# A two-layer graph network: the attention step over three groups, exponentials kept in PSUM, a bias by matrix product

## The chip, the cores and the metric

The kernel runs on one core of a Trainium2 chip. The metric is the device time of one execution in microseconds (us); for the kernel before it is the median of three timed runs. Five engines work side by side on their own instruction streams: TensorE (PE, with its weight loads as PEld), VectorE (DVE), ScalarE (ACT), GpSimd (POOL), and SyncE (SP), which here only starts transfers. SBUF is the on-chip memory, PSUM the small one that TensorE writes its products to.

## What is computed

The input is x, 3125 nodes of 256 features, with 50000 edges sorted by target. Each layer adds to x a graph part and a mixing part, both of the normalised x, and then a feed-forward part. Only the first half of layer 1 matters here:

```python
xn = _layernorm(x)
# graph part: attention over the edges, 4 heads, 64 features
messages = (xn @ Wf.T)[src] * direction[:, 0:1] + (xn @ Wr.T)[src] * direction[:, 1:2]
scores = leaky_relu(einsum('ef,hf->eh', messages, attn), 0.2)
exp_scores = exp(scores - scores.max(axis=0, keepdims=True))
norm = exp_scores / (segment_sum(exp_scores, dst)[dst] + 1e-10)
outs = [segment_sum(messages * norm[:, h:h+1], dst) for h in range(4)]
# mixing part ("Galerkin"): 8 heads of 64, no softmax
q, k, v = split(xn @ Wqkv.T, 3);  k, v = inst_norm(k), inst_norm(v)
dots = einsum('bhnd,bhne->bhde', k, v)
out = einsum('bhnd,bhde->bhne', q, dots) / n
x = x + concat(outs) + (out @ Wout.T + bout)
```

Everything is in float32.

## The kernel before

The 3125 nodes are 25 tiles of 125 (P = 125, NT = 25), in seven chunks (`CHUNKS`) of four, four, four, four, three, three and three tiles. The edges are 391 columns of 128, and `GROUP = 8` columns make a group: 49 groups. The program runs through layer 0's mixing (a dense adjacency that is built by scattering and multiplied, L460), layer 0's feed-forward (a mixture of experts, whose two results per token are added to x at L915, chunk by chunk, two loads and two adds each), layer 1's mixing, and layer 1's feed-forward (another mixture of experts with its own graph attention). Outside of the attention loop a framework that sees what each instruction reads and writes sets the order of each engine's instructions; it does so from the program and a model of costs.

Layer 1's mixing, `layer1_mix`, begins with `layernorm` (per tile `bn_stats` L168 and `bn_aggr` L169 on VectorE; per chunk a Sqrt on ScalarE L170, a reciprocal L171, per tile the normalised row L178 on VectorE, transposes on TensorE L183 and copies on ScalarE L185). `token_matmul` (L191, two products per tile) then makes a table of 136 numbers per node: for each of the two directions 64 message features and 4 head scores. The table `tab1` is written to device memory.

The attention loop goes over the 49 groups and two more iterations. Inside it, for TensorE, VectorE and ScalarE, the order of instructions is the order in which the program issues them (`manual_schedule`); GpSimd's and SyncE's are left to the framework. Iteration i does, in this order:

- `fetch(i+3)`: eight indirect gathers (L51, GpSimd's queue) of table rows, into one of four buffers `g1`;
- `messages(i)`: VectorE makes messages and scores (L1211 to L1215) and the group's maximum per head (L1220), TensorE transposes it (L1222, PSUM tile `psm`);
- `weigh(i-1)`: VectorE multiplies the messages of the group before with the exponential of each head (L1268, 128 x 2048 elements), which ScalarE has written into the 65th column of each head's block in `v`;
- `maximum(i)`: VectorE updates the running maximum (L1229 to L1231), TensorE spreads it over the partitions (L1235);
- `products(i-1)`: TensorE multiplies one-hot matrices of the targets with `v` (L1276), for each window of 125 targets that the group may touch, one PSUM tile `pw` per window, from four buffers. A group touches one to three windows, and so has 8 to 16 columns to multiply;
- `add(i-2)`: VectorE rescales the window's accumulator by how the maximum grew (L1285) and adds `pw` (L1287); for a window met for the first time ScalarE copies it (L1290);
- `ones_of(i)`: VectorE makes the one-hot matrices (L1260); `exponents(i)`: VectorE subtracts the maximum (L1240, L1241), ScalarE makes the exponentials (L1243, and L1245 for the growth).

At the end of every iteration the generator `galerkin` is advanced once by `next(todo, None)`, and so lays the mixing part between the groups. Its steps, one per iteration: the key and value weights are loaded, transposed (L1446, copied at L1447) and centred (L1451 to L1453); then 26 kv steps. Step t normalises tile t-1 (sum of squares L1462, L1463, L1465 on VectorE, Sqrt L1466 on ScalarE, reciprocal L1467 and multiply L1468 on VectorE), adds it into `pdots` (L1470, TensorE, four products), and makes keys and values of tile t (TensorE L191, copies L1480 and squares L1482 on ScalarE). Then come one step for `dots` and the transposed `Wout`, one for `m2` (L1502, L1503), and one for the combined matrix `gm` (L1511, L1513) with the first of seven chunks; a chunk multiplies each tile of xn with `gm` (L191), adds the product to x (L1519, VectorE), and after its last tile adds the bias, spread over all partitions, to the chunk (L1520, VectorE). The remaining six chunks take one step each.

Of the kernel before, what the change touches and what calls it, by code (L numbers as in the profile page):

```python
# [18 lines left out]
D = 256  # L19
P = 125  # L20
NT = 25
# [4 lines left out]
GROUP = 8  # L26
# [62 lines left out]
class Kernel:  # L89
# [1068 lines left out]
    def layer1_mix(self):  # L1158
        nc, tc, a = self.nc, self.tc, self.a
        W, HD = 68, 64  # L1160
        with ExitStack() as m:
            big = m.enter_context(tc.tile_pool(name="l1", bufs=1))
            wk = m.enter_context(tc.tile_pool(name="l1w", bufs=2))
            gp = m.enter_context(tc.tile_pool(name="l1g", bufs=3))
            ps_a = m.enter_context(tc.tile_pool(name="l1pa", bufs=2, space=PSUM))
            ps_c = m.enter_context(tc.tile_pool(name="l1pc", bufs=1, space=PSUM))
            ps_w = m.enter_context(tc.tile_pool(name="l1pw", bufs=4, space=PSUM))
            ps_s = m.enter_context(tc.tile_pool(name="l1ps", bufs=1, space=PSUM))

            xT = big.tile([128, 2, N], F32, name="xT2")  # L1170
# [67 lines left out]
            def exponents(n, s, pb):  # L1238
                big2 = gp.tile([128, 2, 4], F32, name="top_b", bufs=4)
                nc.vector.tensor_copy(big2, pb)  # L1240
                nc.vector.tensor_sub(s[:, :n, :], s[:, :n, :], big2[:, 0:1, :].to_broadcast([128, n, 4]))  # L1241
                v = gp.tile([128, GROUP, 4, HD + 1], F32, name="v1", bufs=2)
                nc.scalar.activation(v[:, :n, :, HD], s[:, :n, :], AF.Exp)  # L1243
                grown = gp.tile([128, 4], F32, name="grown", bufs=4)
                nc.scalar.activation(grown, big2[:, 1, :], AF.Exp)  # L1245
                return big2, grown, v

            def tiles_in(j0, n):

# [14 lines left out]
                    hots.append(hot)  # L1264
                return hots

            def weigh(n, o, v):
                nc.vector.tensor_mul(v[:, :n, :, :HD], o[:, :n, None, :HD].to_broadcast([128, n, 4, HD]),  # L1268
                                     v[:, :n, :, HD:].to_broadcast([128, n, 4, HD]))

            def products(j0, n, v, hots):
                sums = []
# [23 lines left out]
            with tc.manual_schedule(engines={E_.PE, E_.DVE, E_.Activation}):  # L1296
                todo = self.galerkin(big, wk, ps_a, ps_c, xT)
                starts = [(j0, min(GROUP, NJ - j0)) for j0 in range(0, NJ, GROUP)]
                G = len(starts)
                ahead = [fetch(starts[i][0]) for i in range(3)]  # L1300
                msg, exps, summed = {}, {}, {}
                for i in range(G + 2):
                    if i + 3 < G:
                        ahead.append(fetch(starts[i + 3][0]))
                    if i < G:
                        j0, n, g = ahead[i]
                        o, s, pt = messages(j0, n, g)
# [12 lines left out]
                last = exps[G - 1][0]  # L1320
# [14 lines left out]
            for t0, n in CHUNKS:  # L1335
                s = slice(t0, t0 + n)
# [96 lines left out]
    def galerkin(self, big, wk, ps_a, ps_c, xT):  # L1433

        nc, a = self.nc, self.a
        wkv = big.tile([128, 2, 1024], F32, name="wkv")
        for c4 in range(2):
            nat = wk.tile([128, 4, D], F32, name="nat4", bufs=1)  # L1440
# [14 lines left out]

        pc = ps_c.tile([128, 4, 128], F32, name="pdots")
        kvs = {}
        for t in range(NT + 1):
            if t > 0:
                kv, sq = kvs.pop(t - 1)  # L1460
                var = wk.tile([P, 16], F32, name="kv_var")
                nc.vector.tensor_reduce(var, sq, AX.X, OP.add)  # L1462
                nc.vector.tensor_scalar(var, var, 1.0 / 64, LN_EPS, op0=OP.mult, op1=OP.add)  # L1463
                both = wk.tile([P, 8], F32, name="kv_both")
                nc.vector.tensor_mul(both, var[:, 0:8], var[:, 8:16])  # L1465
                nc.scalar.activation(both, both, AF.Sqrt)  # L1466
                nc.vector.reciprocal(both, both)  # L1467
                nc.vector.tensor_mul(kv[:, 8:, :], kv[:, 8:, :], both[:, :, None].to_broadcast([P, 8, 64]))  # L1468
                for hp in range(4):
                    nc.tensor.matmul(pc[:, hp, :],  # L1470
                                     kv[:, 8 + 2 * hp:10 + 2 * hp, :].rearrange("p a b -> p (a b)"),
                                     kv[:, 2 * hp:2 * hp + 2, :].rearrange("p a b -> p (a b)"),
                                     start=(t == 1 and hp == 0), stop=(t == NT and hp == 3),
                                     skip_group_check=True)
# [12 lines left out]
        for s in (slice(0, 64), slice(64, 128)):  # L1487
            nc.vector.tensor_copy(dots[s, :, s], pc[s, :, s])

        woT = big.tile([128, 4, D], F32, name="woT")  # L1490
        nat = wk.tile([128, 2, 512], F32, name="nat4", bufs=1)
        nc.sync.dma_start(nat, a["L1_mix_Wout"].rearrange("(c p) f -> p c f", p=128))
        for cc in range(2):
# [2 lines left out]
                nc.tensor.transpose(pt[:, i, :], nat[:, cc, i * 128:(i + 1) * 128], self.ident)  # L1496
            nc.scalar.copy(woT[:, :, cc * 128:(cc + 1) * 128], pt)
        yield
        m2 = big.tile([128, 4, D], F32, name="m2")
        for hp in range(4):  # L1500
            pm = ps_a.tile([128, D], F32, name="ln_pt")
# [2 lines left out]
        wq = wk.tile([128, 4, D], F32, name="nat4", bufs=1)  # L1504
        nc.sync.dma_start(wq, a["L1_mix_Wqkv"][0:512, :].rearrange("(c p) d -> p c d", p=128))
        yield
        g = big.tile([128, 2, D], F32, name="gm")
        for k in range(2):
            pm = ps_a.tile([128, D], F32, name="ln_pt")
# [1 line left out]
                nc.tensor.matmul(pm, wq[:, hp, k * 128:(k + 1) * 128], m2[:, hp, :],  # L1511
                                 start=(hp == 0), stop=(hp == 3))
            nc.scalar.copy(g[:, k, :], pm)  # L1513
        bout = self.bcast(big, "L1_mix_bout")
        for t0, n in CHUNKS:
            for t in range(t0, t0 + n):
                pm = ps_a.tile([P, D], F32, name="ln_pt")
                self.token_matmul(pm, xT, t, g)
                nc.vector.tensor_add(self.x[:, t, :], self.x[:, t, :], pm)  # L1519
            nc.vector.tensor_add(self.x[:, t0:t0 + n, :], self.x[:, t0:t0 + n, :],  # L1520
                                 bout[:, None, :].to_broadcast([P, n, D]))
            yield


# [386 lines left out]
```

## Time and profile before

| | us |
|---|---|
| timed runs: median (lowest, highest) | 3240.6 (3229.06, 3284.13) |
| profiled execution, its own time | 2833.29 |
| profiled execution, span | 2831.5 |
| mean granted TensorE clock | 0.874 of full speed |
| attention: first messages to last messages | 1632.7 to 2233.7 |

Busy time in some stretches of the profiled execution, with the mean granted clock:

| stretch, us | what runs | PE | DVE | ACT | POOL | clock |
|---|---|---|---|---|---|---|
| 1550 to 1633 | last adds of layer 0, layernorm, table | 27.6 | 35.1 | 17.9 | 9.2 | 0.63 |
| 1700 to 1900 | groups with kv steps | 180.9 | 181.5 | 92.5 | 158.7 | 1.00 |
| 1900 to 2000 | last kv steps, `dots`, `m2`, `gm` | 80.3 | 81.5 | 31.1 | 79.5 | 0.91 |
| 2000 to 2120 | groups with chunks | 81.3 | 67.2 | 4.7 | 70.9 | 0.82 |
| 2120 to 2250 | groups alone | 102.8 | 114.5 | 7.5 | 86.7 | 0.86 |

How to read the lines of a profile: L1268 is line 1268 of the kernel. A group of instructions names its line, engine and operation, then what it writes, an arrow and what it reads, the shape (partitions x elements) and how many there are. A line of a single instruction, or of a run of equal ones, begins with its start and its duration in us, and ends with the engine's idle time just before it and what ended it, in square brackets. A line of waits names who waits, for whom, and the total in us, the number of waits and the longest. The clock digits give the granted TensorE clock in tenths for forty equal slices of the span, 9 being 90% or more. The profiled execution is 407 us shorter than the median of the timed runs.

### The profile page before, as it was taken

To read this page: it belongs to the slowest core of one execution; us is meant where nothing else is said; L and a number is where in the kernel's file an instruction comes from. 1 tells how busy PE (TensorE), PEld (TensorE's weight loads), DVE (VectorE), ACT (ScalarE), POOL (GpSimd) and SP (SyncE) were. 2 spreads that over 40 slices of the span, in tenths; PEclk is the share of its full clock that TensorE was granted. 3 is DMA by queue.
4 is the path that set the end of the run, shared out by engine and by line. 5 is a ranking of instruction groups with operands and counts; after the bars stand their busy time and mean duration, and the time that the engine had idled before them with its cause. 6 is when DMAs were issued, how large, how long until landed. Compare 5 with 4: busy or idle time off the path is not lost. (4 is left out here: it accounts for less than half of the span.)

```text
span 2831.5 us, 26589 instructions
## 1 busy us (share of the span) xinstructions
PE 2184.2 (77%) x9023; PEld 1643.4 (58%) x9023; DVE 1529.5 (54%) x3663; ACT 523.4 (18%) x1051; POOL 1673.8 (59%) x1493
## 2 busy tenths in 40 slices
PE   1761759999976999999998369988668676999900
PEld 1450547876663677888887346665556554666600
DVE  7975598545569501222121479988558841322227
ACT  2320000000011112222221224443000021222300
POOL 4888788773003604666665077777748417777740
PEclk9855869999967999999999679999888878999955
DMA  8920533312401205555553421112111121122242
GB/s 299 382 89 14 115 89 89 87 44 71 112 31 31 74 1 202 191 191 185 183 184 113 105 62 48 48 47 54 46 32 45 27 68 16 25 52 51 58 89 68
DMA packets 179598, 263.46 MB, mean 93 GB/s; under 512 B 54398, under 2 KB 144008, under 8 KB 176193
## 3 DMA queue, kind: packets, MB, share of 16 engines
q1 hardware_dynamic: 121008, 204.78, 23.4%
q0 software_dynamic: 52544, 47.72, 7.4%
q10 hardware_dynamic: 5894, 9.09, 1.0%
q8 instruction: 75, 1.23, 0.2%
q14 instruction: 77, 0.63, 0.1%
HBM read 177.15 MB, written 84.22 MB: 92 GB/s over the span
## 5 line engine op out<-in xcount | busy, mean ns | idle before, releaser
L58 POOL DMA_INDIRECT adj<-ch_sum,ch_place x391 | 513.3, 1313 | 148.3 <-issue 111.5
L51 POOL DMA_INDIRECT g<-tab,t_src x391 | 458.6, 1173 | 222.5 <-issue 109.4
L58 POOL DMA_INDIRECT sorted<-s_rows,pos x256 | 245.9, 960 | 186.7 <-DVE s_rows L1055 118.2
L460 PE MATMUL psum<-sup,adjT 125*125 125x256 f32 x1250 | 292.8, 393 | 52.4 <-DMA adjT<-adj 41.2
L1276 PE MATMUL pw<-v,hot 128*125 128x260 f32 x1244 | 320.5, 420 | 0.0
L51 POOL DMA_INDIRECT G<-tabg,g_src x256 | 254.2, 993 | 79.9 <-issue 70.4
L460 PEld LDWEIGHTS psum<-sup,adjT 125*125 125x125 f32 x1250 | 240.8, 194 | 94.0 <-DMA adjT<-adj 43.3
L1276 PEld LDWEIGHTS pw<-v,hot 128*125 128x125 f32 x1244 | 253.7, 207 | 48.0
L864 PE MATMUL ph<-xs,w 128*128 128x256 f32 x1024 | 231.5, 384 | 8.5 <-issue 6.0
L892 PE MATMUL py<-w,h 128*128 128x256 f32 x1024 | 231.2, 379 | 0.0
L864 PEld LDWEIGHTS ph<-xs,w 128*128 128x128 f32 x1024 | 193.6, 192 | 45.7 <-issue 17.6
L1632 PE MATMUL fpy<-fw,fh 128*125 128x256 f32 x800 | 186.2, 389 | 32.2 <-DVE y L1634 27.1
L892 PEld LDWEIGHTS py<-w,h 128*128 128x128 f32 x1024 | 192.1, 190 | 24.8
L1632 PEld LDWEIGHTS fpy<-fw,fh 128*125 128x125 f32 x800 | 152.2, 192 | 70.1 <-DVE y L1634 28.4
L866 ACT ACTIVATE h<-ph,b 128x256 f32<-128x256 f32 x256 | 121.3, 475 | 366.2 <-PE ph L864 335.8
L1624 PE MATMUL fph<-xT,fw 128*128 128x500 f32 (+1 forms) x448 | 176.4, 543 | 0.3 <-DMA fw<-in_L_ffn_W_dram 0.3
L1030 PE MATMUL pctx<-s_mv,s_ro 128*128 128x256 f32 x512 | 155.4, 415 | 1.9 <-DVE s_mv L1029 1.9
L895 DVE TENSOR_SCALAR yo<-py,own 128x256 f32<-128x256 f32 x64 | 29.6, 481 | 194.0 <-PE py L892 194.0
L58 POOL DMA_INDIRECT slots<-rows,abi x50 | 72.8, 1455 | 100.2 <-DVE r_cum L944 85.2
L463 DVE TENSOR_TENSOR x<-x,psum 125x512 f32<-125x512 f32 (+1 forms) x104 | 69.0, 666 | 109.1 <-PE psum L460 108.9
L1624 PEld LDWEIGHTS fph<-xT,fw 128*128 128x128 f32 x448 | 85.5, 192 | 72.3 <-issue 49.8
L1626 ACT ACTIVATE fh<-fph,cols 128x500 f32<-128x500 f32 (+1 forms) x112 | 70.3, 633 | 297.3 <-PE fph L1624 264.1
(514 smaller groups left out, 3268.8 us busy)
## 6 DMA issues: line engine op xcount, KB each, us to landing
adjT<-adj SPq DMA_DIRECT2D x25, 1367.2 KB
adj<-zero SPq DMA_DIRECT2D x22, 1536.0 KB
w<-in_L_ffn_W1p_dram SPq DMA_DIRECT2D x32, 1024.0 KB
w<-in_L_ffn_W2p_dram SPq DMA_DIRECT2D x32, 1024.0 KB
slots<-empty SPq DMA_DIRECT2D x1, 8448.0 KB
srow<-slots SPq DMA_DIRECT2D x32, 264.0 KB
adj<-ch_sum,ch_place POOLq DMA_INDIRECT x391
g<-tab,t_src POOLq DMA_INDIRECT x391
```

The lines of the kernel that those rows point to most:

```text
L51: nc.gpsimd.indirect_dma_start(out=out, out_offset=None, in_=table, in_offset=bass.IndirectOffsetOnAxis(ap=idx, axis=0))
L58: return nc.gpsimd.indirect_dma_start(out=table, out_offset=bass.IndirectOffsetOnAxis(ap=idx, axis=0), in_=rows, in_offset=None, **kw)
L460: nc.tensor.matmul(pm[:, i, :], mats[b][:, (a0 + i) * P:(a0 + i + 1) * P], sup[:, b, :], start=(b == b0), stop=(b == b0 + n - 1))
L463: nc.vector.tensor_add(xs, xs, pm[:, :m, :])
L864: nc.tensor.matmul(ph, w1[:, k, f * 128:(f + 1) * 128], xs[:, k, :], start=(k == 0), stop=(k == 1))
L866: nc.scalar.activation(h[:, f, :], ph, AF.Gelu, bias=b1[:, f:f + 1])
L892: nc.tensor.matmul(py, h[:, f, i * 128:(i + 1) * 128], w2[:, f, :], start=(f == 0), stop=(f == FC - 1))
L1030: nc.tensor.matmul(p1, ro[:, f - f0, :], mv, **st)
L1276: nc.tensor.matmul(pw.rearrange("p h c -> p (h c)"), hot[:, i - i0, :], v[:, i, :, :].rearrange("p h c -> p (h c)"), start=(i == i0), stop ...
L1624: nc.tensor.matmul(ph[:, :n * P], w1[:, k, f * 128:(f + 1) * 128], xT[:, k, t0 * P:(t0 + n) * P], start=(k == 0), stop=(k == 1))
L1626: nc.scalar.activation(hs[:, f, :n * P], ph[:, :n * P], AF.Gelu, bias=self.col("L1_ffn_b1", ei * FC + f))
L1632: nc.tensor.matmul(py, hs[:, f, i * P:(i + 1) * P], w2[:, f, :], start=(f == 0), stop=(f == FC - 1))
```

## The change

Three edits are made in `layer1_mix` and `galerkin`.

- The Galerkin part of a tile spans three groups. The generator yields more often and is advanced twice per iteration, a second time between `weigh(i-1)` and `maximum(i)`. In iteration t+1, at that middle place, tile t-2 gets its reciprocal and multiply; at the end, tile t-1 gets its sum of squares and Sqrt, tile t-2 is added into `pdots`, and tile t is projected. The steps after kv, which came one per iteration, still do so, with the first chunks one iteration later than before. There are three buffers of `kv` instead of two, and two of `kv_sq` instead of one.
- `exponents` writes the exponentials a second time, into the PSUM tile `ev`, and `weigh` reads them there; `v` still gets its 65th column, which the products use. The bank for `ev` is taken from `pw`, which has three buffers instead of four.
- The bias is loaded as one row and added in PSUM by a product of a row of ones with it, one per tile. Two tiles share a PSUM tile, and one VectorE instruction adds both to x.

In the changed kernel the order of VectorE's and ScalarE's instructions ahead of the attention, which the framework sets, is another too: the adds of layer 0's result (L915) and the steps of `layernorm` take turns chunk by chunk, where before all adds came first. The instructions are the same.

```diff
-            ps_w = m.enter_context(tc.tile_pool(name="l1pw", bufs=4, space=PSUM))
+            ps_w = m.enter_context(tc.tile_pool(name="l1pw", bufs=3, space=PSUM))
+            ps_e = m.enter_context(tc.tile_pool(name="l1pe", bufs=1, space=PSUM))
...
                 v = gp.tile([128, GROUP, 4, HD + 1], F32, name="v1", bufs=2)
+                ev = ps_e.tile([128, GROUP, 4], F32, name="ev")
+                nc.scalar.activation(ev[:, :n, :], s[:, :n, :], AF.Exp)
                 nc.scalar.activation(v[:, :n, :, HD], s[:, :n, :], AF.Exp)
...
-            def weigh(n, o, v):
+            def weigh(n, o, v, ev):
                 nc.vector.tensor_mul(v[:, :n, :, :HD], o[:, :n, None, :HD].to_broadcast([128, n, 4, HD]),
-                                     v[:, :n, :, HD:].to_broadcast([128, n, 4, HD]))
+                                     ev[:, :n, :, None].to_broadcast([128, n, 4, HD]))
...
-                        weigh(starts[i - 1][1], msg[i - 1][0], exps[i - 1][2])
+                        weigh(starts[i - 1][1], msg[i - 1][0], *exps[i - 1][2:])
+                    next(todo, None)
                     if i < G:
                         pb = maximum(pt)
...
         nc, a = self.nc, self.a
+        yield
...
-        for t in range(NT + 1):
-            if t > 0:
-                kv, sq = kvs.pop(t - 1)
+        for t in range(NT + 2):
+            if t > 1:
+                kv, both = kvs[t - 2]
+                nc.vector.reciprocal(both, both)
+                nc.vector.tensor_mul(kv[:, 8:, :], kv[:, 8:, :], both[:, :, None].to_broadcast([P, 8, 64]))
+            yield
+            if 0 < t <= NT:
+                kv, sq = kvs[t - 1]
                 var = wk.tile([P, 16], F32, name="kv_var")
                 nc.vector.tensor_reduce(var, sq, AX.X, OP.add)
                 nc.vector.tensor_scalar(var, var, 1.0 / 64, LN_EPS, op0=OP.mult, op1=OP.add)
                 both = wk.tile([P, 8], F32, name="kv_both")
                 nc.vector.tensor_mul(both, var[:, 0:8], var[:, 8:16])
                 nc.scalar.activation(both, both, AF.Sqrt)
-                nc.vector.reciprocal(both, both)
-                nc.vector.tensor_mul(kv[:, 8:, :], kv[:, 8:, :], both[:, :, None].to_broadcast([P, 8, 64]))
+                kvs[t - 1] = kv, both
+            if t > 1:
+                kv = kvs.pop(t - 2)[0]
                 for hp in range(4):
...
             if t < NT:
-                kv = wk.tile([P, 16, 64], F32, name="kv")
+                kv = wk.tile([P, 16, 64], F32, name="kv", bufs=3)
...
-                sq = wk.tile([P, 16, 64], F32, name="kv_sq", bufs=1)
+                sq = wk.tile([P, 16, 64], F32, name="kv_sq")
...
-        bout = self.bcast(big, "L1_mix_bout")
+        bout = big.tile([1, D], F32, name="bout")
+        nc.sync.dma_start(bout, a["L1_mix_bout"][None, :])
         for t0, n in CHUNKS:
-            for t in range(t0, t0 + n):
-                pm = ps_a.tile([P, D], F32, name="ln_pt")
-                self.token_matmul(pm, xT, t, g)
-                nc.vector.tensor_add(self.x[:, t, :], self.x[:, t, :], pm)
-            nc.vector.tensor_add(self.x[:, t0:t0 + n, :], self.x[:, t0:t0 + n, :],
-                                 bout[:, None, :].to_broadcast([P, n, D]))
+            for t1 in range(t0, t0 + n, 2):
+                m = min(2, t0 + n - t1)
+                pm = ps_a.tile([P, 2, D], F32, name="ln_pt")
+                for i in range(m):
+                    for k in range(2):
+                        nc.tensor.matmul(pm[:, i, :], xT[:, k, (t1 + i) * P:(t1 + i + 1) * P], g[:, k, :],
+                                         start=(k == 0), stop=False)
+                    nc.tensor.matmul(pm[:, i, :], self.full[0:1, :P], bout, start=False, stop=True)
+                xs = self.x[:, t1:t1 + m, :]
+                nc.vector.tensor_add(xs, xs, pm[:, :m, :])
+            yield
             yield
```

More of the change, by code (lines that the diff above doesn't have):

```diff
@@ L1245, in exponents @@
                 nc.scalar.activation(grown, big2[:, 1, :], AF.Exp)
-                return big2, grown, v
+                return big2, grown, v, ev
             def tiles_in(j0, n):
@@ L1472, in galerkin @@
                                      kv[:, 2 * hp:2 * hp + 2, :].rearrange("p a b -> p (a b)"),
-                                     start=(t == 1 and hp == 0), stop=(t == NT and hp == 3),
+                                     start=(t == 2 and hp == 0), stop=(t == NT + 1 and hp == 3),
                                      skip_group_check=True)
             if t < NT:
-                kv = wk.tile([P, 16, 64], F32, name="kv")
+                kv = wk.tile([P, 16, 64], F32, name="kv", bufs=3)
                 for i in range(2):
@@ L1498, in galerkin @@
         yield
+        yield
         m2 = big.tile([128, 4, D], F32, name="m2")
@@ L1506, in galerkin @@
         yield
+        yield
         g = big.tile([128, 2, D], F32, name="gm")
@@ L1513, in galerkin @@
             nc.scalar.copy(g[:, k, :], pm)
[L1514 removed]
+        bout = big.tile([1, D], F32, name="bout")
+        nc.sync.dma_start(bout, a["L1_mix_bout"][None, :])
         for t0, n in CHUNKS:
[L1516 to L1521 removed]
+            for t1 in range(t0, t0 + n, 2):
[8 more added lines that the diff above has]
+                nc.vector.tensor_add(xs, xs, pm[:, :m, :])
+            yield
             yield
```

## Prediction

> **What bounds the kernel now.** I read the page's head first (span, busy time, granted clock in 40 slices of 70.8 us), then the attention stage of layer 1, which is what the edit touches.
>
> ```profile
> span 2831.5 us, 26589 instructions
> PE 2184.2 (77%) x9023; PEld 1643.4 (58%) x9023; DVE 1529.5 (54%) x3663; ACT 523.4 (18%) x1051; POOL 1673.8 (59%) x1493
> PEclk9855869999967999999999679999888878999955
> ```
>
> No engine bounds the whole, so each part of the change is priced where it lies. I read three stretches: the way into the attention (1550 to 1633 us), the kv groups (1643 to about 1960) and the seven chunks that add the Galerkin result to x (about 2000 to 2120).
>
> In the way in, the list of single instructions shows VectorE (DVE) first making all fourteen adds of layer 0's result, each waiting for a load, and only then the layernorm; then comes one long wait for the first gather.
>
> ```profile
> 1556.48 1.22 DVE L915 TENSOR_TENSOR x<-x,w 125x1024 f32<-125x1024 f32 x1 [1.00 <-DMA w<-y]
> ...
> 1579.46 0.75 DVE L168 BATCH_NORM_STATS2 ln_st<-x 125x6 f32<-125x256 f32 x2
> ...
> 1632.73 0.73 DVE L1211 TENSOR_TENSOR msg<-g,t_dir 128x544 f32<-128x544 f32 x1 [33.10 <-DMA g<-tab,t_src]
> ```
>
> In the kv groups the waits list shows TensorE (PE) waiting for the normalised kv tile (total us, times, longest), and the instructions show one such group followed by one without:
>
> ```profile
> PE pdots L1470 <- DVE kv L1468: 15.1, 12, 2.3
> ```
>
> ```profile
> 1917.77 4.65 PE L1276 MATMUL pw<-v,hot 128*125 128x260 f32 x20
> ...
> 1924.68 1.13 PE L1470 MATMUL pdots<-kv 125*128 125x128 f32 x8 [2.26 <-DVE kv L1468]
> ...
> 1931.93 7.28 PE L1276 MATMUL pw<-v,hot 128*125 128x260 f32 x32
> ```
>
> A group with few one-hot products (20 records, 4.65 us) leaves PE waiting; one with 32 (7.28 us) doesn't, and there DVE waits for PE instead. In the chunks both engines take turns:
>
> ```profile
> 2026.37 3.62 PE L191 MATMUL ln_pt<-gm,xT 128*125 128x256 f32 x16
> 2030.02 0.42 DVE L1519 TENSOR_TENSOR x<-x,ln_pt 125x256 f32<-125x256 f32 x1 [0.44 <-PE ln_pt L191]
> 2030.47 1.22 DVE L1520 TENSOR_TENSOR x<-x,b_L_mix_bout 125x1024 f32<-125x1024 f32 x1
> ```
>
> The next group's messages (L1211) start after L1520, so what a chunk takes is added to its group.
>
> [...]beside the weighing L1268[...] a gather took 1.89 us instead of 0.95.
>
> ```profile
> 1708.40 0.95 POOL L51 DMA_INDIRECT g<-tab,t_src  x1 [0.31 <-issue]
> 1708.41 2.30 DVE L1268 TENSOR_TENSOR v<-msg,v 128x2048 f32<-128x2048 f32 x1
> 1709.65 1.89 POOL L51 DMA_INDIRECT g<-tab,t_src  x1 [0.30 <-issue]
> ```
>
> [...]426 ns (L1287, from PSUM) against 410 (L1285, from SBUF) at 260 elements[...]. [...]the granted clock is 1.00 between 1700 and 1900 us and 0.82 in the chunks, and the same eight kv projections took 3.60 us in one group and 5.29 in another.
>
> **The change, part by part.** The sum is made on the profiled execution: span 2831.5 us, own time 2833.29.
>
> *Way in to the attention.* Not in the diff, but the order of the changed kernel's instructions has it: DVE takes each chunk's L915 adds and then that chunk's layernorm, instead of all adds first. L915 ran from 1554.26 to 1579.4 and waited 13.4 us for loads, of which the first 3.8 come before any work. The layernorm (20.2 us, 1579.46 to 1599.64) can fill the other 9.6. The adds' own work is 25.1 − 9.6 = 15.5, the layernorm 20.2, and I leave 2.5 for seven Sqrt round trips to ScalarE (ACT) that nothing covers any longer: 1554.3 + 38.2 = 1592.5 instead of 1599.64, −7.1 (bounds 0 and −9.6). Behind it all moves along: transposes, table, first gather. PE's wcat products run after the last transpose (1601.4) in both orders.
>
> *kv in three groups.* Per kv tile, DVE's reciprocal and multiply (L1467, L1468) move from the end of a group to the middle of the next, PE's pdots to that group's end, and the generator takes a step twice per group. No operation is added. PE's wait of 15.1 us in 12 groups goes; late next is DVE, which in each such group gets back only what it idles itself: its wait at the next L1229 plus some 0.37 us for L1466's Sqrt. Taking the smaller of the two pair by pair gives 2.2 us in some, about 0.5 in most, 9.0 in sum: −9.0 (bounds 0 and −15.1, the whole wait). In groups with 32 products DVE does L1468 inside its wait for PE (1.83 us at 1931.09). ACT's order changes too, but it is 46% busy from 1700 to 1900 us and waits for PE. The load of Wout and the later ones (SP's queue) go out one group later, with half a group of cover more.
>
> *ev in PSUM.* A second Exp per group on ACT: 49 × about 0.26 us (the first one's size) = 12.7 us, in idle ACT time; the weighing needs it last, but comes a whole message step later (bounds 0 and 12.7). L1268 then reads PSUM: 49 × 0.01 (L1287 against L1285)[...]; I take +0.5. [...]a gather group falls from about 11.7 us to 8 × (0.95 + 0.30) = 10.0. But a gather landed 0.5 to 0.9 us before its use in groups 3 to 21, and nobody waits, except at the first use and at the last two groups (0.72 and 1.32 us against 0.18 elsewhere): −1.7.
>
> *One PSUM buffer fewer for the products (4 to 3).* L1276 writes one per window; only three groups have three windows, and there PE must wait for the add (L1287) of the group before: some 0.65 + 0.2 us each, with all later PE work queued behind: +2.0 (bounds 0 and 4).
>
> *Bias by product.* DVE loses L1520: 4 × 1.224 + 3 × 0.958 = 7.8 us, all on the turn-taking path. PE gains 25 products with one row of weights, 50 records. No such row exists; the nearest, L817, has 9 rows and 425 ns against 379 for full ones, so few rows are no cheaper:
>
> ```profile
> L817 PE MATMUL py<-b,gT x50: 374/425/477, 911.0 to 1072.4; 9*125 9x256 f32 x50
> ```
>
> At the chunk's pace (16 records in 3.62 us, DVE's adds 0.865 us apart for four) a record costs 0.216: 50 × 0.216 = +10.8. The last add of a four-token chunk is now a pair: 0.687 us (L463, 125x512 from PSUM) against 0.422, 4 × 0.265 = +1.1. Sum −7.8 + 10.8 + 1.1 = +4.1 (bounds −6.7 if the rows are free, +15 at half clock). The bias load shrinks from 125 rows to one, off the path.
>
> Sum: −7.1 − 9.0 + 0.5 − 1.7 + 2.0 + 4.1 = −11.2, so a span of 2820 and an own time of 2822.1. The median of the timed runs is 3240.6, 407 us above the profiled execution, and nothing in the profile shows where. Unscaled that is 3229.4, scaled by 1.144 it is 3227.8: I say 3229.
>
> **The rivals.**
> - *Nothing is gained* (the waits only change names; the new order meets the same loads): 0.5 + 2 + 4.1 − 1.7 = +5, 3245. For it: DVE was 91% busy from 1700 to 1900. Against: the 9.6 us between the adds are plainly empty.
> - *Slower, by the clock*: the 407 us are TensorE at half clock. The bias products then cost 50 × 0.43 = 21.5, and a light group's 20 records 9.3 us, longer than the 7.1 us from L1235 until kv is ready, so PE never waited and kv gains nothing: 21.5 − 7.8 + 1.1 + 0.5 + 2 − 7.1 = +10, 3251. It decides below a clock of 4.65 / 7.1 = 0.65. For it: the slices show 0.5 to 0.6 after idle stretches. Against: the mean was 0.87.
> - *Faster, by the gathers*: in the timed runs the gathers bound the attention. It decides once a gather and its pause take over 11.67 / 8 = 1.46 us (11.67 is a kv group's period). Then the 1.66 us that each of 26 groups gets back count: −43 more, 3186. For it: gathers land under 0.9 us ahead. Against: no wait for them is seen there.
> - *Much slower, by the broadcast from PSUM*: L1268 reads each ev 64 times; if that halves its rate, 49 × 2.2 = +108, hence −11 + 108 = +97, 3337. It decides from about 0.5 us more per L1268. For it: no row before has such a read. Against: L1287 above.
>
> **How the numbers follow.** Likeliest 0.55, nothing gained 0.13, half clock 0.15, gathers 0.12, PSUM rate 0.05. Two per cent, 65 us, is about what a measurement of this kernel can tell from no change (its three runs lie 1.7% apart). The range goes from 3186 (the gathers' case) to 3265 (half clock[...]), which leaves out the PSUM case and a few tails. Over 2% faster needs the gathers' case and more: 0.04; slower is the PSUM case: 0.05.
>
> **What would show it.** DVE's last L178 some 38 us after the first L915 (45 before); no wait of pdots for kv; gathers beside the weighing at 0.95 and a group of them near 10 us; [...]chunk groups about 0.6 us longer; PE waiting for a buffer only in three groups. A weighing at 4.5 us, or waits of L1211 for gathers after the first group, would make the prediction wrong.

## The result, and the profile after

The changed kernel takes 3319.93 us (median of four), the kernel before 3234.83: ratio 1.0297, 95% interval 1.0242 to 1.0352. It is slower, where 0.4% faster was forecast.

The runs met the kernel before in two conditions of the chip, 2830 to 2832 us in two sets of runs and 3205 to 3244 in the others, the comparison above among them, while the profile of before that the prediction was made from (2833 us) shows the first. Below they are called the free and the slowed chip, but these are names for a condition, not for two chips: the record numbers the chips of the five sets below 9, 13, 10, 5 and 9, and number 9 was free in the first set and slowed in the fifth. All runs of a set fell in the same condition; what brings it about isn't known.

The page of the changed kernel, on the slowed chip:

```profile
span 3296.8 us, 26725 instructions
PE 2278.7 (69%) x9073; PEld 1682.5 (51%) x9073; DVE 1521.4 (46%) x3645; ACT 529.2 (16%) x1100; POOL 1583.0 (48%) x1493
PEclk9955765589997899999998679998777776979965
```

Against the profile of before, which is from the free chip, TensorE is by the record busy 95 us longer and ScalarE 6 (with 49 exponentials more), VectorE and GpSimd less; much of the added span, 465 us, is waiting. The waits list between 1870 and 2590 us has what replaced PE's wait for kv:

```profile
DVE top L1230 <- remote: 97.9, 9, 30.3
DVE x L1540 <- PE ln_pt L1538: 77.2, 14, 13.3
ACT kv L1491 <- remote: 64.8, 8, 35.6
...
DVE msg L1212 <- DMA g<-tab,t_src: 33.2, 3, 32.8
```

"remote" stands where the event that ends a wait matches no recorded end of an instruction ("issue", further down, where the profile shows no wait, or one for something that by its record was over long before). Here is such a wait, in the second kv group, one line each for the weighing, the projections, the transpose, ScalarE's copy of the projections and VectorE's maximum:

```profile
1915.63 2.28 DVE L1271 TENSOR_TENSOR v<-msg,ev 128x2048 f32<-128x2048 f32 x1
...
1917.55 3.60 PE L191 MATMUL ln_pt<-wkv,xT 128*125 128x512 f32 x8
...
1920.98 0.27 PE L1223 MATMUL psm<-ident,mx 128*4 128x128 f32 x1
...
1948.94 1.07 ACT L1491 COPY kv<-ln_pt 125x512 f32<-125x512 f32 x2 [35.57 <-remote]
1949.03 0.28 DVE L1230 TENSOR_REDUCE top<-psm 4x1 f32<-4x128 f32 x1 [30.29 <-remote]
```

By the record the transpose ended at 1921.25; the maximum, which waits for it alone, starts 27.8 us later, and so does the copy of projections that TensorE had started before. The two engines that wait for TensorE were let go within 0.09 us of each other, so I take it that TensorE itself was later than its records say, and call this a stall of TensorE. In the stage with the dense adjacency (L460), which no edit touches, it is seen plainly. A stretch of 50 us there (columns: busy time and count of PE, PEld, DVE, ACT, POOL, then clock, DMA share, GB/s), first in the changed kernel:

```profile
500.00:550.00 50.00, 10.49 (x18) 5.10 (x18) 5.73 (x19) 0.00 (x0) 37.90 (x40) 0.50 0.02 0
```

and in the profile of before on the free chip:

```profile
500.00:550.00 50.00, 50.00 (x233) 43.62 (x232) 24.72 (x52) 0.00 (x0) 38.42 (x39) 1.00 0.19 45
```

18 records of products instead of 233 (a product leaves two: a tile's four into `pdots` are eight records in the prediction's lines of 1924.68), at a recorded clock of 0.50. Waits of VectorE and ScalarE over 1 us that end in "remote" tell the two conditions apart: over the whole span their union is 0 us in each of the nine profiles from the free chip, and 357 to 572 us in the eleven from the slowed one.

### The profile page after: what moved, and what is told of

It is laid out like the page before. It is cut to its first block, busy times and chain, and to the rows that moved or that the text cites. A ratio compares the mean times of both kernels' runs of the same rounds, so it can differ in the third digit from the quotient of the medians.

```text
span 3296.8 us, 26725 instructions
## 1 busy us (share of the span) xinstructions
PE 2278.7 (69%) x9073; PEld 1682.5 (51%) x9073; DVE 1521.4 (46%) x3645; ACT 529.2 (16%) x1100; POOL 1583.0 (48%) x1493
## 3 DMA queue, kind: packets, MB, share of 16 engines
q1 hardware_dynamic: 120880, 204.65, 20.4%
## 5 line engine op out<-in xcount | busy, mean ns | idle before, releaser
L51 POOL DMA_INDIRECT g<-tab,t_src x391 | 399.5, 1022 | 355.9 <-DVE score L1216 178.5
L58 POOL DMA_INDIRECT adj<-ch_sum,ch_place x391 | 484.7, 1240 | 155.0 <-issue 119.3
L460 PE MATMUL psum<-sup,adjT 125*125 125x256 f32 x1250 | 319.3, 406 | 206.8 <-issue 138.8
L460 PEld LDWEIGHTS psum<-sup,adjT 125*125 125x125 f32 x1250 | 247.2, 200 | 268.2 <-issue 160.2
L1279 PE MATMUL pw<-v,hot 128*125 128x260 f32 x1244 | 340.5, 438 | 0.2
L1279 PEld LDWEIGHTS pw<-v,hot 128*125 128x125 f32 x1244 | 266.5, 218 | 55.3 <-issue 1.4
L1652 PE MATMUL fpy<-fw,fh 128*125 128x256 f32 x800 | 209.9, 420 | 76.1 <-ACT fh L1646 29.3
L1652 PEld LDWEIGHTS fpy<-fw,fh 128*125 128x125 f32 x800 | 165.2, 210 | 126.6 <-issue 35.3
L1644 PE MATMUL fph<-xT,fw 128*128 128x500 f32 (+1 forms) x448 | 184.2, 559 | 37.2 <-ACT fh L1646 32.5
L170 ACT ACTIVATE ln_rs<-ln_mv,eps 125x4 f32<-125x4 f32 (+1 forms) x28 | 7.6, 296 | 802.0 <-DVE ln_mv L169 802.0
```

The lines of the kernel that those rows point to most:

```text
L51: nc.gpsimd.indirect_dma_start(out=out, out_offset=None, in_=table, in_offset=bass.IndirectOffsetOnAxis(ap=idx, axis=0))
L58: return nc.gpsimd.indirect_dma_start(out=table, out_offset=bass.IndirectOffsetOnAxis(ap=idx, axis=0), in_=rows, in_offset=None, **kw)
L460: nc.tensor.matmul(pm[:, i, :], mats[b][:, (a0 + i) * P:(a0 + i + 1) * P], sup[:, b, :], start=(b == b0), stop=(b == b0 + n - 1))
L1279: nc.tensor.matmul(pw.rearrange("p h c -> p (h c)"), hot[:, i - i0, :], v[:, i, :, :].rearrange("p h c -> p (h c)"), start=(i == i0), stop ...
L1644: nc.tensor.matmul(ph[:, :n * P], w1[:, k, f * 128:(f + 1) * 128], xT[:, k, t0 * P:(t0 + n) * P], start=(k == 0), stop=(k == 1))
L1652: nc.tensor.matmul(py, hs[:, f, i * P:(i + 1) * P], w2[:, f, :], start=(f == 0), stop=(f == FC - 1))
```

## The experiments

The stages of their profiles in us, worked out from the starts of the same instructions in each: the way in from the first L915 to the first messages; kv from there to the end of the last `m2` (one group later in the three-group order); rest from there to the start of the last messages; L460 from the first to the last of its products; ffn the same for layer 1's feed-forward. "kv stalls" is the union of VectorE's and ScalarE's waits over 1 us that end in "remote", within kv.

| run | chip | way in | kv | rest | L460 | ffn | kv stalls |
|---|---|---|---|---|---|---|---|
| before (again) | free | 78.7 | 359.1 | 241.2 | 506.2 | 406.0 | 0 |
| split | free | 70.8 | 362.6 | 231.7 | 505.5 | 406.0 | 0 |
| ev | free | 79.2 | 364.0 | 241.0 | 504.6 | 406.0 | 0 |
| bias | free | 79.0 | 359.2 | 252.5 | 506.0 | 405.2 | 0 |
| before (before_t) | slowed | 78.1 | 362.0 | 255.9 | 685.1 | 535.5 | 5.6 |
| pairs | slowed | 78.7 | 358.5 | 247.8 | 712.0 | 525.6 | 0 |
| fill | slowed | 78.2 | 403.4 | 241.3 | 694.7 | 537.9 | 0 |
| split (split_b) | slowed | 70.4 | 405.0 | 232.7 | 708.0 | 524.7 | 40.6 |
| ev (ev_b) | slowed | 78.4 | 393.3 | 267.4 | 710.7 | 540.3 | 31.4 |
| changed (the profile above) | slowed | 70.8 | 437.8 | 266.7 | 708.0 | 528.8 | 98.3 |
| changed (after_again) | slowed | 71.0 | 414.5 | 259.4 | 706.8 | 527.5 | 66.4 |
| changed (after_s) | slowed | 70.9 | 437.9 | 266.5 | 722.9 | 547.6 | 97.2 |
| early | slowed | 73.9 | 413.7 | 247.4 | 700.1 | 524.3 | 75.1 |
| slack | slowed | 70.4 | 431.4 | 263.1 | 735.3 | 540.8 | 110.2 |

`split_ev` isn't in the table: its one profile is of an execution of 3306.6 us, 1.9% above the median of its runs. The kv column doesn't hold all of the attention's stalls: before_t and pairs have one of 19.4 and one of 14.2 us in the chunks.

**First set, free chip: the kernel before, and each part alone.**

> The kernel before, unchanged, for a second profile and for the spread. Theory A (TensorE is slowed in stretches that come with the execution, in both kernels, and the one profile of the kernel before happened to have few of them): time about 3235 us, ratio 1.000 within 0.5%, and this profile has a span near 3230 with TensorE at half clock for about 1000 us instead of 713, single matmuls far apart in the L460 stage, and an attention of 650 to 700 us instead of 601 from first to last messages. Theory B (the slow stretches belong to the changed kernel): the profile stays near 2830 us with an attention of 601 us.

> Only the Galerkin part over three groups (kv buffers 3, kv_sq 2, two steps per iteration); ev and the bias as before. The prediction's steps: kv -9 us, the way in -7 us, so a ratio of 0.995. Theory C (the whole loss comes from this part[...]): ratio 1.02 to 1.03, half clock well above that of the kernel before run alongside.

> Only the exponentials in PSUM, the weighing from there, and three PSUM buffers for the products instead of four. The prediction's steps: +0.5 +2.0 -1.7, ratio 1.000. Rival (an order of the engines that leaves TensorE idle, or the second Exp on the path to the weighing): ratio 1.005 to 1.02, with waits of L1271 for L1245 or of L1276 for a buffer. Weighing 2.28 us per group and gathers at 0.95 beside it by both.

> Only the bias by product, in pairs of tiles. The prediction's step: +4 us, ratio 1.001. Rival, from the profile of the changed kernel, whose chunk groups took 172 us against 148: +24 us, ratio 1.007, with the adds to x waiting for the product L1524 for 70 to 80 us in all instead of 51.

The edits: `again` has none; `split` has only the `galerkin` and `next(todo, None)` lines of the diff that is shown, without the bias; `ev` only those of `ev`, `weigh` and the two pools; `bias` only the last block, with one `yield` per chunk.

Measured: again 1.0000 (0.9992 to 1.0009), split 0.9946 (0.9932 to 0.9960), ev 0.9996 (0.9987 to 1.0005), bias 1.0047 (1.0031 to 1.0063), beside 2832.0 us. The second profile of before is the first over again (kv 359.1, no stall), and no part costs 3%: the loss does not lie in the work of any part alone. With the three-group order PE no longer waits for kv, but VectorE waits for gathers instead. The waits of `split` and of `again`, 1620 to 2240 and 1630 to 2255 us:

```profile
DVE msg L1211 <- DMA g<-tab,t_src: 46.3, 25, 32.7
```

```profile
DVE msg L1211 <- DMA g<-tab,t_src: 35.7, 9, 32.8
...
PE pdots L1470 <- DVE kv L1468: 15.1, 12, 2.3
```

Outside the first group that is 13.6 us instead of 2.9. In `ev` the gathers beside the weighing stay short, 0.95 us in the lines below against 1.89 in the profile of before, and the weighing isn't slower from PSUM (2278 ns against 2294). First the 48 full weighings of before (busy us, mean ns of one, idle time before), then those of `ev`, then three single lines of `ev`:

```profile
L1268 DVE TENSOR_TENSOR v<-msg,v 128x2048 f32<-128x2048 f32 x48 | 110.1, 2294 | 0.0
```

```profile
L1271 DVE TENSOR_TENSOR v<-msg,ev 128x2048 f32<-128x2048 f32 x48 | 109.3, 2278 | 0.0
```

```profile
1729.72 0.95 POOL L51 DMA_INDIRECT g<-tab,t_src  x1 [0.30 <-issue]
1729.75 2.28 DVE L1271 TENSOR_TENSOR v<-msg,ev 128x2048 f32<-128x2048 f32 x1
1730.98 0.94 POOL L51 DMA_INDIRECT g<-tab,t_src  x1 [0.30 <-issue]
```

In `bias` a chunk shows what a product with one row of weights costs:

```profile
2028.15 1.13 PE L1522 MATMUL ln_pt<-gm,xT 128*125 128x256 f32 x4
2029.21 0.69 PE L1524 MATMUL ln_pt<-bout,full 1*125 1x256 f32 x2
2029.83 1.13 PE L1522 MATMUL ln_pt<-gm,xT 128*125 128x256 f32 x4
2029.94 0.69 DVE L1526 TENSOR_TENSOR x<-x,ln_pt 125x512 f32<-125x512 f32 x1 [9.74 <-PE ln_pt L1524]
...
2033.30 0.69 DVE L1526 TENSOR_TENSOR x<-x,ln_pt 125x512 f32<-125x512 f32 x1 [2.67 <-PE ln_pt L1524]
```

Two tiles take 3.36 us, one 1.68, where the adds were 0.865 apart before: 0.815 for two records, 0.41 each. (The two take 0.62 from the start of the first to the next product; the four full ones before them take 1.06 instead of 0.865.) 25 x 0.815 = 20.4, less 7.8 for L1520, is +12.6; the chunks' eight groups took 12.0 more in the trace and the kernel 13.1, between the 4 and the 24 that were expected.

**Second set, slowed chip: the changed kernel, and parts of the bias edit.**

> The changed kernel itself, beside the kernel before, as the three parts were run: alone they gave 0.9946, 0.9996 and 1.0047. Theory A (the 2.97% of the first comparison come from a chip in a state in which TensorE finishes late, and not from the work itself): the parts add up, 2832 - 15 - 1 + 13 = 2829 us, ratio 0.999, or down to 0.995 where ev makes the gathers short and so gives the three-group order what it waits for in them (13.6 us); no stretch in which VectorE waits for a TensorE that by its record had ended. Theory D (the parts harm each other): ratio near 1.03 here as well, 2915 us.

> The changed kernel with the bias as before (spread over the partitions, added by VectorE per chunk). If the order and ev help each other by way of the gathers: 2832 - 15 - 1 - 10 = 2806 us, ratio 0.991, with VectorE waiting for gathers only at the first group. If not: the plain sum, 0.994. By Theory D near 1.02.

> The kernel before with the chunks' tiles in pairs in one PSUM tile and one add per pair, but the bias as before and no product for it. Tells the two halves of the bias part's +13 us apart. If the one-row products cost what the bias run's trace shows (1.68 us per tile against 0.905, so 25 x 0.775 = +19.4) and the bias add removed gives 7.8 back, the pairs are +1.5 us: ratio 1.0005. If the pairing is what costs: +5 to +10 us, ratio 1.002 to 1.0035.

> The changed kernel without the products for the bias: VectorE adds the bias to x in seven instructions at the start of the attention, where it waits some 33 us for the first gather, and the chunks add tile by tile. 7.8 us less than the split_ev kernel: 2798 us by the helping theory, ratio 0.988; no less than split_ev if the adds delay the first messages.

`after_again` is the changed kernel, `split_ev` the same with the bias block of the kernel before.

```diff
# early: instead of the products for the bias
                 todo = self.galerkin(big, wk, ps_a, ps_c, xT)
+                bout = self.bcast(big, "L1_mix_bout")
+                for t0, n in CHUNKS:
+                    nc.vector.tensor_add(self.x[:, t0:t0 + n, :], self.x[:, t0:t0 + n, :],
+                                         bout[:, None, :].to_broadcast([P, n, D]))
# pairs: in the kernel before
-            for t in range(t0, t0 + n):
-                pm = ps_a.tile([P, D], F32, name="ln_pt")
-                self.token_matmul(pm, xT, t, g)
-                nc.vector.tensor_add(self.x[:, t, :], self.x[:, t, :], pm)
+            for t1 in range(t0, t0 + n, 2):
+                m = min(2, t0 + n - t1)
+                pm = ps_a.tile([P, 2, D], F32, name="ln_pt")
+                for i in range(m):
+                    self.token_matmul(pm[:, i, :], xT, t1 + i, g)
+                xs = self.x[:, t1:t1 + m, :]
+                nc.vector.tensor_add(xs, xs, pm[:, :m, :])
```

Measured beside 3205.3 us: after_again 1.0186 (1.0140 to 1.0232), split_ev 1.0120 (1.0082 to 1.0158), pairs 0.9986 (0.9964 to 1.0007), early 1.0116 (1.0082 to 1.0150). The order and `ev`, each neutral or better alone on the free chip, lose together here (`split_ev`), and the bias is only some 0.7% of the loss (1.0186 against 1.0120). The pairs cost nothing. `early`, forecast 7.8 us below `split_ev`, can't be told from it. Theory A held in that the chip is slowed; it fell in that the loss comes from the chip alone: the pairs run has the chip's stalls in L460 and ffn, but none in kv. Theory D, that the parts harm each other, forecast near 1.03 and near 1.02 for `split_ev`, and neither was reached.

**Third set, slowed chip: what brings the stalls into kv.**

> Only ev in PSUM, once more, for a chip that slows TensorE (the kernel before takes about 3200 us there) as in the runs of the changed kernel, where VectorE waited 60 to 100 us in the kv groups for TensorE work that by its record had ended. Theory P (those stalls come with a TensorE that is left without pauses beside busy VectorE, ScalarE and gathers): ratio 1.000, kv groups as before (about 358 us up to the last m2), no such waits of the maximum L1230 there. Theory Q (they come with VectorE reading PSUM while TensorE writes it): ratio 1.01 to 1.015 and such waits. Should the chip be one that doesn't slow TensorE: 1.000 by both, as it was.

> Only the Galerkin part over three groups, once more, for such a chip. Theory P: slower by the stalls but less than with ev, as waits for gathers still leave TensorE pauses: ratio 1.003 to 1.012, and waits of the maximum L1229 for TensorE of 20 us or more in the kv groups. Theory Q: faster as on the other chip, 0.995, and none. On a chip that doesn't slow TensorE: 0.9946 as it was.

> The kernel before, with the first half of each kv projection made twice (the first result overwritten): 4 records of 0.43 us more per kv group on TensorE, 43 us in all, some of it in the pauses that TensorE has in the groups with few products. Theory P on a chip that slows TensorE: the stalls of the changed kernel appear in the old order too, kv groups at 358 + 30 + 40 or more, ratio above 1.02. Theory Q: the work alone, 25 to 40 us, ratio 1.008 to 1.012, no stalls there.

> The changed kernel with the bias as before, and the kv products into pdots left out but for the first and the last tile: 1.1 us of TensorE work less in 24 groups, so that TensorE has pauses again while VectorE, ScalarE and the gathers do as in the three-group order. It leaves out the sum over the tiles in the Galerkin part. Theory P: the stalls shrink to under half of what the split_ev kernel showed (70 us of waits of the maximum for TensorE), and the time is at or under that of the kernel before. Theory Q: they stay at 70 us, ratio 1.005 to 1.01.

```diff
# fill: in the kernel before
-                    self.token_matmul(pk, xT, t, wkv[:, :, 512 * i:512 * i + 512])
+                    for _ in range(2 - i):
+                        self.token_matmul(pk, xT, t, wkv[:, :, 512 * i:512 * i + 512])
# slack: in split_ev
-                for hp in range(4):
+                for hp in range(4 if t in (2, NT + 1) else 0):
```

Measured beside 3244.0 us: ev_b 1.0100 (1.0061 to 1.0139), split_b 0.9955 (0.9933 to 0.9977), fill 1.0017 (0.9995 to 1.0039), slack 1.0236 (1.0151 to 1.0321). Theory P, a TensorE without pauses, fell twice: more work on it (fill) brought no stall into kv, and less (slack, which leaves out the kv products of all tiles but the first and the last) left more stalls there than any other profile of the table. (In fill the groups grew with the work, so its TensorE was hardly denser than before, busy for 86% of kv against 85% in before_t; it is slack that decides.) Theory Q forecast the ratios of ev_b and split_b, but split_b has 40.6 us of kv stalls of its own, so PSUM reads are not their only cause. Neither theory has the times of slack (1.0236 in four runs, 1.010 at most by Q) and fill: the kv of fill is 41 us longer than in before_t and that of split_b 43, yet one kernel is 0.2% slower and the other 0.5% faster than the kernel before. Either other stages give this back, or the kernel before had stalls in kv in this set too; no profile of it was taken there. What `ev` adds shows best at the first kv group, where ev_b and before_t issue the same instructions in the same order but for the second exponential. First ev_b, then before_t, on the slowed chip:

```profile
1909.86 2.27 DVE L1271 TENSOR_TENSOR v<-msg,ev 128x2048 f32<-128x2048 f32 x1
1911.26 3.60 PE L191 MATMUL ln_pt<-wkv,xT 128*125 128x512 f32 x8
...
1925.56 0.59 ACT L1483 COPY kv<-ln_pt 125x512 f32<-125x512 f32 x1 [17.88 <-issue]
...
1940.30 0.28 DVE L1230 TENSOR_REDUCE top<-psm 4x1 f32<-4x128 f32 x1 [28.17 <-remote]
```

```profile
1897.09 2.28 DVE L1268 TENSOR_TENSOR v<-msg,v 128x2048 f32<-128x2048 f32 x1
1898.37 3.60 PE L191 MATMUL ln_pt<-wkv,xT 128*125 128x512 f32 x8
1900.29 0.59 ACT L1480 COPY kv<-ln_pt 125x512 f32<-125x512 f32 x1 [5.55 <-PE ln_pt L191]
```

The copy comes 14.3 us after the projections' start instead of 1.9. A stall of 25 us or more in the first two kv groups is in the six profiles of the table on the slowed chip that have the `ev` edit (three of the changed kernel, early, ev_b, slack) and in none of the four without it (before_t, pairs, fill, split_b); the same six stall again, by 15 us or more, in the last groups, after the chunks, and the four don't. This speaks for the edit as a whole: with the reads of PSUM come a second exponential and one PSUM buffer fewer, and on the slowed chip no run has one without the others.

**Fourth set, free chip: what in `ev` it is.**

> The kernel before, unchanged, for its profile on a chip that slows TensorE. If the stalls in the kv groups belong to the change: none there, 358 us from the first messages to the last m2, as in the pairs and fill runs. If they fall on any order and those two had luck: 20 to 60 us of waits for TensorE work that by its record had ended, 380 to 420 us. On a chip that doesn't slow TensorE: 2832 us and 358.

> As ev, but the second exponential goes to a tile in SBUF, and the weighing reads that; the products have four PSUM buffers as before. If the reads of PSUM bring the stalls: as the kernel before, ratio 1.000, kv groups as in before_s. If the second exponential does: 1.01, as ev on such a chip. On a chip that doesn't slow TensorE: 1.000, with gathers of 1.9 us beside the weighing again.

> As ev, with the second exponential written to PSUM and three buffers for the products, but the weighing reads its factor from SBUF as before, and nothing reads ev. If the reads of PSUM, or the gathers that they leave free, bring the stalls: ratio 1.000. If the write to PSUM or the missing buffer does: 1.01.

> The Galerkin part over three groups, ev as before, and the bias added to x by VectorE in its wait for the first gather (no product, no pairs). The split gave 0.9946 and 0.9955; 7.8 us less in the chunks make 0.992 on either chip. If the chunks' adds hide in waits for TensorE anyway: 0.995.

```diff
# ev_sbuf: in ev, with four buffers pw
-                ev = ps_e.tile([128, GROUP, 4], F32, name="ev")
+                ev = gp.tile([128, GROUP, 4], F32, name="ev", bufs=2)
# ev_unread: in ev
-                                     ev[:, :n, :, None].to_broadcast([128, n, 4, HD]))
+                                     v[:, :n, :, HD:].to_broadcast([128, n, 4, HD]))
```

Measured beside 2830.1 us: before_s 1.0001 (0.9993 to 1.0010), ev_sbuf 1.0003 (0.9994 to 1.0011), ev_unread 1.0015 (1.0007 to 1.0023), split_early 0.9940 (0.9927 to 0.9953). The free chip can't answer on stalls; so what in `ev` sets off TensorE's stalls stays open: the PSUM reads themselves, the gathers of 0.95 us instead of 1.89 beside them, the second exponential or the missing buffer. It does price the PSUM buffers: kv is 363.9 with three (ev_unread) and 358.7 with four (ev_sbuf), so 5.2 us, though the two differ too in where the second exponential is written. The version `split_early` (the `split` edits and the `early` lines) beats the kernel before, but hardly `split`: the rest of the attention is 6.2 us shorter, and 3.5 us come back in the way in, where the first four adds of the bias (from 1585.27 us) stand ahead of the layernorm's last rows (L178 at 1591.05).

**Fifth set, slowed chip: the profile of before that was missing.**

> The changed kernel. On a chip that doesn't slow TensorE (kernel before at 2830 us): the parts' sum, -15 - 1 + 13 = -3 us, ratio 0.999; down to 0.995 if ev takes away the waits for gathers (13.6 us) that the three-group order had alone. On a chip that slows it (3200 us): 1.02 to 1.03 once more.

> The kernel before, for its profile. On a chip that slows TensorE: no stalls in the kv groups and 358 us from the first messages to the last m2, if they belong to the change; 20 to 60 us of them if they fall on any order. On one that doesn't: 2830 us, 358, no stalls.

Measured beside 3228.6 us: after_s 1.0207 (1.0148 to 1.0267), before_t 0.9997 (0.9974 to 1.0019). In before_t kv is 362.0 us with 5.6 of stalls, 3 us from the free chip's; in after_s 437.9 with 97.2. The longest waits for TensorE in the attention of after_s, and the longest "remote" one of before_t:

```profile
DVE x L1540 <- PE ln_pt L1538: 77.0, 14, 13.2
ACT kv L1491 <- remote: 69.8, 7, 17.0
DVE top L1230 <- remote: 67.5, 7, 20.3
```

```profile
DVE x L1519 <- remote: 21.1, 2, 19.4
```

So the slowed chip costs the kernel before 385 us of span (3215.6 against 2830.8), of which 309 lie in L460 and ffn (685.1 - 506.2 = 179 and 535.5 - 406.0 = 130), which both kernels pay, and only 18 in kv and rest; the others lie elsewhere, most of them ahead of L460, which starts 36 us later. Over the whole span the waits that end in "remote" are 438 us in before_t and 521 in after_s: 83 more, beside 93 us more of span. The two reach the first L915 within 1 us of each other. The change carries the stalls into the attention, which was nearly free of them.

## Why the prediction was wrong, step by step

- **The way in, -7.1.** Right: 78.1 to 70.9 in the fifth set, -7.2; on the free chip 78.7 to 70.8. It comes with `split`, whose whole gain on the free chip, 14.4 us, is near the 16.1 forecast for this step and the next.
- **kv in three groups, -9.0.** PE's wait went as said. On the free chip `split` from first to last messages takes 594.3 us instead of 600.4, -6.1 of the 9.0, because the gathers, at 11.6 to 12 us for most groups beside an SBUF weighing, come next, and not VectorE: the 13.6 us of waits for them are what the prediction named as a sign of being wrong. In after_s such waits are 0.6 us after the first group; but the stalls give the gathers time there, so this doesn't show what would come next without stalls. On the slowed chip `split` alone still gains 0.45% by time, though its profile has kv stalls; where that is made up isn't shown.
- **ev, +0.5 and -1.7.** The weighing was mis-sized: 2278 ns against 2294, so it gained 0.8 us where 0.5 was to be lost. Gathers beside it took 0.95 us (`ev`, 1729.72 and 1730.98 us), against 1.89 beside L1268 in the profile of before. That they would was the author's estimate: the profile of before has no weighing from PSUM to show it. The range's upper end, 3265, is an estimate beyond the 3251 of the half clock. With the next term, the part measured 0.9996 on the free chip.
- **One PSUM buffer fewer, +2.0.** Three waits at 0.85 us make 2.6, not the 2.0 that was put in. In `ev` and ev_unread TensorE waits for a buffer three times, as forecast, but only 0.68 us each, and the waits end at ScalarE's L1485 and not at VectorE's add. The stage still grows by 5.2 (ev_unread against ev_sbuf), above the bound of 4.
- **Bias by product, +4.1.** Mis-sized term: a one-row record adds 0.41 us and not the chunk's 0.216; +13.1 in all. The nearest case, L817 with nine rows, didn't show it. That +13.1 is within the upper bound of 15 is luck: that bound was for a half clock, at 0.43 us a record, and in the stretch shown above the full records go at 0.27 (four in 1.06).
- **The step that failed** is the last of the sum, "Unscaled that is 3229.4, scaled by 1.144 it is 3227.8": the 407 us between profile and timed runs were taken as a constant or a factor, the same on either kernel. They go with stalls of TensorE in stages of their own, and the change alters which stages have them: +76 us in kv and +11 in the rest (fifth set, where the medians are 77 us apart), in a sum that had no term for it. By time the parts on the slowed chip are 0.9955 (split), 1.0100 (ev), and with both 1.0120; their product is 1.0055, and the 0.65% between is hardly more than the intervals of the three leave room for. With the bias it is 1.0186 to 1.0297. On the free chip the parts' product is 0.9989, some -3 us where -11 was forecast, most of the difference being the bias; the changed kernel itself wasn't met there. What sets off the stalls in the attention stays open.
- **The rivals.** "Nothing is gained" forecast +5 us; on the free chip the parts come to about nothing (-3), but not for its reason, as the way in and kv did gain. "Slower, by the clock" had the sign and TensorE, but priced a half clock at +10; a stalled TensorE is far slower, with one record of a product every 2.8 us (below). That idleness lowers the clock was not shown: in the profile of before it is recorded at 0.50 from 1630 to 1650 us, where a wait of 17.4 us without a product ends, and at 1.00 from 1660 to 1700, where TensorE is busy for 94%; the two only go together there. "Faster, by the gathers" fell: the kernel before hardly waits for them in the timed condition either (2.5 us in before_t after the first group). "Much slower, by the broadcast from PSUM" fell as priced, since the weighing keeps its rate; a stall of TensorE that comes with `ev` was not in it.

## What to carry to other kernels

When the profiled execution and the timed runs are 14% apart, as here, they may not be in the same condition: find out first which engine the missing time belongs to and where, since a change can bring it into a stage that was nearly free of it. Price parts one at a time, and in both conditions: `split` is worth 0.5% in each, `ev` nothing in one and -1% in the other. And cost a small product by a measurement of one among its neighbours: here neither the rows nor the neighbours' own pace gave its price.

## What the runs showed of the hardware that was not expected

TensorE was far slower here than the recorded clock of 0.50 accounts for. Single records of L460's products in before_t on the slowed chip:

```profile
500.44 0.59 PE L460 MATMUL psum<-sup,adjT 125*125 125x256 f32 x1 [2.21 <-issue]
503.24 0.59 PE L460 MATMUL psum<-sup,adjT 125*125 125x256 f32 x1 [2.21 <-issue]
506.04 0.59 PE L460 MATMUL psum<-sup,adjT 125*125 125x256 f32 x1 [2.21 <-issue]
```

They are 2.80 us apart, against 42 in 9.23 us at 499.81 us in the profile of before on the free chip, and the recorded clock is 0.50. In all slowed profiles TensorE's weight loads and products keep falling into one pace, 1.40 us from one start to the next: 28 to 194 such steps in each, most of them in L460, and 1 to 4 in each free one. The stalls in kv keep about this pace, so I take them for the same thing: in after_s, ScalarE's copies of the first projections (1905.48 and 1915.28 us) come 13.6 us after TensorE's start and 9.8 us later, for four records of products each, so 3.4 and 2.4 us a record. The recorded clock of 0.50 alone doesn't explain 2.80 us: at half the free chip's pace of 0.22 us a record (9.23 us for 42) I estimate 0.44. Either the record of the clock is wrong there, or something other than the clock held TensorE up; the runs don't tell which. They show a slowing by more than ten (2.80 against 0.22), and a TensorE that is busy for only 10.6 of the 100 us from 500 to 600 in before_t. What sets it off isn't known: in L460 it came with every kernel on the slowed chip, in kv with the `ev` edit, and less with the three-group order alone.
